# Layer 1 of a graph network: one column of source rows in seven selected by TensorE from node rows in SBUF in place of a gather

## The chip, the cores and the metric

The kernel runs on one core of a Trainium2 chip. Times are device microseconds of one execution; the median of ten executions before the change is 16345.49 us (16343.41 to 16347.37).

## The reference, cut to what matters

12500 nodes with 32 features, 400000 edges (src, dst), the edges sorted by dst. Three attention layers run over the edges, then a layer norm, then an edge network with a maximum over each node's edges, and a second layer norm. One attention layer is

```python
h = (x @ W.T).reshape(n, heads, ch)
a_s = (h * att_s[None]).sum(-1)
a_d = (h * att_d[None]).sum(-1)
logits = jax.nn.leaky_relu(a_s[src] + a_d[dst], neg_slope)
m = jax.ops.segment_max(logits, dst, num_segments=n)
ex = jnp.exp(logits - m[dst])
denom = jax.ops.segment_sum(ex, dst, num_segments=n)
alpha = ex / (denom[dst] + 1e-16)
out = jax.ops.segment_sum(alpha[:, :, None] * h[src], dst, num_segments=n)
```

with 2 heads of 16 channels in layers 1 and 2 and one head of 32 in layer 3. Layers 1 and 2 are followed by an elu and a clip at 3. What this case is about is `h[src]` and `a_s[src]`: for every edge, the row of its source node.

## The kernel before

The edges lie in dst order over 128 partitions, 3125 to a partition. Column t of a tile is edge t of every partition. The nodes are numbered p * 98 + c: 98 to a partition.

In front of the layers the kernel computes the rows of layer 1 for all nodes into `tb` (L354 to L364; 32 features, two logits, and the places of the node's last and first edge, 36 floats in all), writes them to `table1` in DRAM (L390), and finds each node's first and last edge with gathers of `found` in groups of up to 28 columns (L367 to L374). `empties` (L557) writes the rows of nodes without edges; it reads the biases.

`attention(li, idx)` goes through the edges in 54 chunks: 50 of 60 columns and the last of 48, 32, 29 and 16. For each chunk it

- gathers the source rows, one indirect DMA on POOL's queue for each column (L666 to L668, issued by the helper at L68), 128 rows a time, into a tile `g` from a pool of 4 buffers; in layer 1 from `table1`
- copies the places out of `g` (L683, L684), forms the logits (L695 to L698) and running maxima (L704) along the edges of a partition
- forms weights on ACT into `small_p` (L715), multiplies the rows by them (L723), and runs a segmented sum with scans over `gf` (L734)
- writes the sums (L736 to L739), divides by the denominator kept in `den`, adds the bias (`divided`, L494 to L501), and in layers 1 and 2 applies the elu and multiplies by the next layer's weights in blocks of 16 columns (`finish`, L510 to L534: L523 and L525 on DVE, L528 and L529 on PE, L531 and L532 on DVE), and writes the rows of the next layer's table (L744, L748)

What the scans hand from chunk to chunk stays in SBUF (`old`). After the last chunk of a layer the partitions' ends are merged (L751 to L784); layers 1 and 2 also issue 49 scatters of x each on POOL there (`move`, L624). `edge_network` (L805) has the same chunks, with gathers into `xs` at L834.

PSUM has eight tiles of 512 floats a partition. Before the change layer 1 uses `fixed` (biases in columns 0 to 127, `node_p` in 256 to 353 during the setup), `small_p` (weights in columns 0 to 119, `den` from 128), two for `rx`, one each for `pe` and `pa`, two for `ph`.

The instructions of an engine run in the order that the program was laid out in before it ran. This order isn't that of the source: independent instructions are put between dependent ones. Waits come from the tiles that instructions write and read.

Of the kernel before, what the change touches and what calls it, by code (L numbers as in the profile page):

```python
# [11 lines left out]
I32 = mybir.dt.int32  # L12
# [11 lines left out]
@with_exitstack  # L24
def gnn_resnorm_kernel(ctx: ExitStack, tc: tile.TileContext, a: dict, out: bass.AP):


# [36 lines left out]
    def bcast(ap, shape):  # L64
        return ap.to_broadcast(shape)
# [9 lines left out]
    def node_rows(table):  # L75
        return table[0:NN, :].rearrange("(p c) w -> p c w", c=NC)
# [4 lines left out]
    def empty_rows(table):  # L81
        return table[E:E + NN, :].rearrange("(p c) w -> p c w", c=NC)

    groups = [(c0, min(28, NC - c0)) for c0 in range(0, NC, 28)]

# [17 lines left out]
    gstack = ctx.enter_context(ExitStack())  # L103
    gpool = gstack.enter_context(tc.tile_pool(name="g", bufs=4, side="right"))
    early = ctx.enter_context(ExitStack())
    dpool = early.enter_context(tc.tile_pool(name="dst", bufs=1, side="right"))
    dst_i = dpool.tile([P, TE], I32, name="dst_i")
    nc.sync.dma_start(out=dst_i, in_=by_partition(a["dst"]))
    x0 = runs.tile([P, NC, D], F32, name="x0")
    nc.vector.memset(x0[96:P, REST:, :], 0.0)  # L110
    for p0, p1 in PIECES:
# [19 lines left out]
                   allow_small_or_imprecise_dtypes=True)  # L131
    fixed = ctx.enter_context(tc.tile_pool(name="fixed", bufs=1, space=PSUM)).tile([P, 512], F32, name="fixed")
    own = const.tile([P, 1], F32, name="own")
    nc.gpsimd.iota(own, pattern=[[1, 1]], base=E + NN, channel_multiplier=1,
                   allow_small_or_imprecise_dtypes=True)
    zeros = const.tile([P, 1250], F32, name="zeros")
    nc.vector.memset(zeros, 0.0)
# [57 lines left out]


    table1 = dram.tile([NN, D + 4], F32, name="table1")
    table_d = dram.tile([NN, 2], F32, name="table_d")
# [9 lines left out]
    def clear(table, part=0, parts=1):  # L208
        flat = edge_rows(table).rearrange("p t w -> p (t w)")
        k = TE * table.shape[1] // parts  # L210
        z = next(z for z in range(1250, 0, -1) if k % z == 0)
        tc.keep_in_program_order(
            nc.sync.dma_start(out=flat[:, part * k:part * k + k].rearrange("p (k z) -> p k z", z=z),
                              in_=bcast(zeros[:, None, :z], [P, k // z, z])))
# [82 lines left out]
    runs2 = ctx.enter_context(tc.tile_pool(name="runs2", bufs=1))  # L297
    cont = runs2.tile([P, TE + 1], F32, name="cont")
    src_last = runs2.tile([P, TE], I32, name="src_last")
    src_first = runs2.tile([P, TE], I32, name="src_first")  # L300
# [13 lines left out]
    with tc.tile_pool(name="seg", bufs=1) as sp, tc.tile_pool(name="rowsp", bufs=2) as rp, \  # L314
# [51 lines left out]

        for c0, n in groups:  # L367
            rows = rp.tile([P, 28, SB], I32, name="found")
            for c in range(n):
                gather(rows[:, c, :], dst_d, find_i[:, c0 + c:c0 + c + 1])  # L370
            less = rp.tile([P, 28, SB], BF16, name="less")[:, :n, :]
            nc.vector.tensor_tensor(less, rows[:, :n, :], bcast(node_p[:, c0:c0 + n, None], [P, n, SB]), op=ALU.is_lt)
            nc.vector.tensor_reduce(r[:, c0:c0 + n], less, axis=AX.X, op=ALU.add)
            nc.vector.tensor_add(first[:, c0:c0 + n], first[:, c0:c0 + n], r[:, c0:c0 + n])  # L374
# [9 lines left out]
        for col, place, index in ((D + 3, first, first_i), (D + 2, last, last_i)):  # L384
# [4 lines left out]
            nc.vector.tensor_copy(index, place)  # L389
        nc.sync.dma_start(out=node_rows(table1), in_=tb)  # L390

        nc.vector.memset(cont[:, 0:1], 0.0)
# [109 lines left out]

    def finish(li, pool, psum, den, v, n, hb=1):

        y = pool.tile([P, D * T], F32, name="y")[:, :D * n].rearrange("p (f t) -> p f t", t=n)
        divided(li, y, den, v, n)
# [10 lines left out]
        for b in range(0, n, TB):  # L517
# [7 lines left out]
            nc.vector.transpose(blocks(yt), yb.rearrange("p f t -> p t f"))  # L525
            ph = psum.tile([P, TB * D], F32, name="ph", bufs=hb)[:, :w]
            pa = psum.tile([P, TB * D], F32, name="pa")[:, :w]
            nc.tensor.matmul(ph, lhsT=w_bd, rhs=yt, start=True, stop=True)  # L528
            nc.tensor.matmul(pa, lhsT=a_bd, rhs=yt, start=True, stop=True)  # L529
            at = pool.tile([P, TB, D], F32, name="at")[:, :nt, :]  # L530
            nc.vector.transpose(tb[:, b:b + nt, :D], blocks(ph))  # L531
# [18 lines left out]
    def finish3(pool, psum, den, v, x, n):  # L550

        y = psum.tile([P, D * 64], F32, name="y3")[:, :D * n].rearrange("p (f t) -> p f t", t=n)
        divided(3, y, den, v, n)
        nc.vector.tensor_add(x, x, y.rearrange("p f t -> p t f"))
        layernorm(pool, den[:, 2 * T:], x, n)

    def empties():  # L557

        for table, r0 in (*((t, E + NN) for t in tables.values()), (gives[2], E), (gives[3], E)):
            w = (ROWS - r0) // P * table.shape[1]  # L560
            nc.sync.dma_start(out=table[r0:, :].rearrange("(p c) w -> p (c w)", p=P), in_=zeros[:, :w])
        with tc.tile_pool(name="empty", bufs=2) as ep, tc.tile_pool(name="emptyps", bufs=1, space=PSUM) as eps:
            for li in (1, 2):
# [15 lines left out]
    def turned(ap, rev):  # L579
        return ap[:, ::-1] if rev else ap  # L580
# [48 lines left out]
    def attention(li, idx):  # L629
# [9 lines left out]

        with tc.tile_pool(name=f"s{li}", bufs=2) as sp, tc.tile_pool(name=f"f{li}", bufs=2) as fp:  # L640
            if li > 1:
# [17 lines left out]
            with tc.tile_pool(name=f"ps{li}", bufs=1, space=PSUM) as psp, \  # L659
                    tc.tile_pool(name=f"fps{li}", bufs=1, space=PSUM) as fps:  # L660

                small_p = psp.tile([P, 512], F32, name="small_p")
                den = small_p[:, 128:]
                old = None
                for c, (t0, n) in enumerate(todo):
                    g = gpool.tile([P, T * (D + 4)], F32, name="g")[:, :n * w].rearrange("p (t w) -> p t w", w=w)  # L666
                    for t in range(n):
                        gather(g[:, t, :], table, idx[:, t0 + t:t0 + t + 1])  # L668
                    (ad, xr) = loaded
# [42 lines left out]
                    nc.vector.tensor_sub(lg, lg, mx[:, :, cur])  # L712
                    rx = psp.tile([P, heads, 512], F32, name="rx", bufs=3 - heads)
                    wt = small_p[:, :heads * n].rearrange("p (h t) -> p h t", t=n)
# [3 lines left out]
                    v = gf[:, :gw * (n + 1)].rearrange("p (f t) -> p f t", t=n + 1)  # L718
                    for h in range(heads):
                        nc.scalar.activation(  # L720
                            rx[:, h, :FS * (n + 1)].rearrange("p (k t) -> p k t", t=n + 1),
                            bcast(rr[:, h:h + 1, :], [P, FS, n + 1]), AF.Exp)
                        nc.vector.tensor_mul(v[:, h * wd:h * wd + ch, cur].rearrange("p f t -> p t f"),  # L723
                                             g[:, :, h * ch:(h + 1) * ch], bcast(wt[:, h, :, None], [P, n, ch]))
                        nc.scalar.copy(v[:, h * wd + ch, cur], wt[:, h, :])  # L725
                    if c == 0:
                        nc.vector.memset(v[:, :, carry:carry + 1], 0.0)
                    else:
                        nc.vector.tensor_copy(v[:, :, carry:carry + 1], old[0])
                    for h in range(heads):  # L730
                        for f in range(0, wd, FS):
                            k = min(FS, wd - f) * (n + 1)
                            o = (h * wd + f) * (n + 1)
                            nc.vector.tensor_tensor_scan(turned(gf[:, o:o + k], rev), turned(rx[:, h, :k], rev),  # L734
                                                         turned(gf[:, o:o + k], rev), 0.0, op0=ALU.mult, op1=ALU.add)
                    rows = sp.tile([P, T, gw + heads], F32, name="rows")[:, :n, :]  # L736
                    nc.scalar.copy(rows[:, :, :gw], v[:, :, cur].rearrange("p f t -> p t f"))  # L737
# [4 lines left out]
                    if li < 3:  # L742
                        tb, ta = finish(li, fp, fps, den, v[:, :, cur], n, hb=2)
                        nc.sync.dma_start(out=edge_rows(gives[li + 1])[:, t0:t0 + n, :], in_=ta)  # L744
                    else:
                        finish3(fp, fps, den, v[:, :, cur], xr, n)
                        tb = xr
# [57 lines left out]
    def edge_network(tag, in_order):  # L805


        with tc.tile_pool(name=f"in{tag}", bufs=2) as ip, tc.tile_pool(name=f"gx{tag}", bufs=4) as gp, \
                tc.tile_pool(name=f"v{tag}", bufs=2) as vp, tc.tile_pool(name=f"t{tag}", bufs=2) as tp, \
                tc.tile_pool(name=f"pf{tag}", bufs=1, space=PSUM) as pfp, \  # L810
                tc.tile_pool(name=f"ph{tag}", bufs=1, space=PSUM) as php:
            small_p = pfp.tile([P, 512], F32, name="small_p")
            todo = list(chunks(True))
# [17 lines left out]
            for c, (t0, n) in enumerate(todo):  # L831
                xs = gp.tile([P, T, D], F32, name="xs")
                for t in range(n):
                    gather(xs[:, t, :], tables[4], src_last[:, t0 + t:t0 + t + 1])  # L834
                xd, ea = loaded
# [57 lines left out]
                old = (xft[:, :, 0], first_v)  # L893
                z = vp.tile([P, T, D], F32, name="z", bufs=1)[:, :n, :]
                for f in range(0, D, FS):
# [62 lines left out]
```

## Time and profile before

| | us |
|---|---|
| median of 10 runs | 16345.49 |
| the profiled execution | 16347.18 |
| its span, first to last instruction | 16344.7 |
| gathers of layer 1 | 302.8 to 4234.2 |
| first and last landing of a chunk in layer 1 (L683) | 406.7, 4235.8 |
| first gather of layer 2 | 4300.2 |

By stage, from the window view: microseconds of the stretch, and busy microseconds of each engine.

| stretch | length | PE | DVE | ACT | POOL | granted clock |
|---|---|---|---|---|---|---|
| layer 1, 300 to 4235 | 3935 | 594.1 | 1474.2 | 808.6 | 2954.2 | 0.56 |
| layer 2, 4300 to 8205 | 3905 | 581.9 | 1412.9 | 789.4 | 2952.1 | 0.57 |
| layer 3, 8270 to 12180 | 3910 | 0.0 | 1387.4 | 503.2 | 2951.0 | 0.50 |
| edge network, 12222 to 16200 | 3978 | 1531.2 | 2394.0 | 734.4 | 2948.8 | 0.68 |
| one pitch of layer 1, 1969.2 to 2044.1 | 74.9 | 12.2 | 28.1 | 15.6 | 56.6 | 0.57 |

POOL's busy time is the issue of gathers and leaves out some 0.3 us between two of them. PE, DVE and ACT are the matrix, vector and scalar engines; PEld is PE's weight load, SP the queue of plain DMAs. The granted clock is that of PE, as a share of full speed. In a timeline line the columns are start, duration, engine, line of the kernel, operation, output and inputs, and in brackets the idle time before it and what ended it.

### The profile page before, as it was taken

How to read it: one execution, taken by the hardware profiler on the slowest of the kernel's cores; microseconds unless marked ns; L12 is line 12 of the kernel's file. 1: busy time of each engine (PE TensorE's matmuls, PEld its weight loads, DVE VectorE, ACT ScalarE, POOL GpSimd, SP SyncE). 2: the span in 40 equal slices, each digit the busy share in tenths (PEclk: the TensorE clock that was granted, in tenths of full speed). 3: DMA queues.
4: the chain of work that ended last, by engine and by line, in shares of the span. 5: the costliest groups of instructions: out<-in, count | busy, mean ns of one | idle time of the engine just before them, and what ended most of it. 6: DMA issues, size and time to landing. Idle time of an engine off the chain costs nothing.

```text
span 16344.7 us, 42394 instructions
## 1 busy us (share of the span) xinstructions
PE 2762.3 (17%) x5140; PEld 1118.3 (7%) x5140; DVE 6834.1 (42%) x9700; ACT 2898.9 (18%) x3835; POOL 12192.9 (75%) x12921
## 2 busy tenths in 40 slices
PE   0111111111111111111100000000003433334342
PEld 0000000000000000000000000000001111111110
DVE  2434333333334333333333333333335666665654
ACT  0212222121212122221211111111111111111111
POOL 6777777777777777777777777777767777777775
PEclk5555555555555555555555555555556666666676
DMA  4222222211111111111112222222222222222221
GB/s 60 76 55 73 55 58 71 55 48 43 43 41 47 41 47 41 44 44 41 47 49 56 51 58 51 56 53 56 53 57 59 66 66 64 67 65 64 69 63 42
DMA packets 580809, 897.64 MB, mean 55 GB/s; under 512 B 286270, under 2 KB 490237, under 8 KB 567069
## 3 DMA queue, kind: packets, MB, share of 16 engines
q1 hardware_dynamic: 167116, 665.01, 11.3%
q0 software_dynamic: 413088, 226.62, 9.6%
q10 hardware_dynamic: 304, 3.20, 0.1%
q14 instruction: 259, 2.12, 0.0%
q8 instruction: 42, 0.69, 0.0%
HBM read 390.67 MB, written 503.27 MB: 55 GB/s over the span
## 4 chain that ended last, share of the span: by engine, by line
POOL 71%; issue 23%; DMA 3%; DVE 1%; PE 0%; ACT 0%; POOLq 0%; DVEq 0%; ACTq 0%
POOL g L68 52%; POOL xs L68 17%; DMA g<-table,src_i 1%; DMA g<-table,src_first 1%; DMA g<-table,src_last 1%; DMA xs<-table,src_last 1%; POOL give L72 1%; POOL so L68 1%; POOL x_e L72 1%; PE ph L877 0%; DMA s<-sums,at_i 0%; PE pv L883 0%; DVE vf L887 0%; DVE z L803 0%; ACT xd L889 0%
## 5 line engine op out<-in xcount | busy, mean ns | idle before, releaser
L68 POOL DMA_INDIRECT g<-table,src_i x3125 | 2951.8, 945 | 979.9 <-issue 938.8
L68 POOL DMA_INDIRECT g<-table,src_last x3125 | 2950.7, 944 | 952.4 <-issue 937.5
L68 POOL DMA_INDIRECT xs<-table,src_last x3125 | 2948.6, 944 | 955.0 <-issue 936.2
L68 POOL DMA_INDIRECT g<-table,src_first x3125 | 2950.0, 944 | 952.4 <-issue 937.5
L697 DVE TENSOR_TENSOR lg<-g,af 128x60 f32<-128x60 f32 (+4 forms) x270 | 59.4, 250 | 4410.7 <-DMA g<-table,src_first 2327.0
L528 PE MATMUL ph<-yt,w_bd 128*128 128x512 f32 (+2 forms) x840 | 665.1, 887 | 3418.1 <-DVE yt L525 3412.1
L529 PE MATMUL pa<-yt,a_bd 128*128 128x512 f32 (+2 forms) x840 | 640.1, 857 | 3320.8 <-DVE at L532 3320.6
L877 PE MATMUL ph<-xt,wb_bd 128*128 128x512 f32 (+2 forms) x832 | 467.1, 646 | 2415.7 <-DVE xt L870 2415.7
L683 DVE CAST src_last<-g 128x60 int32<-128x60 f32 (+4 forms) x54 | 11.9, 221 | 2057.1 <-DMA g<-table,src_i 2057.1
L738 ACT COPY rows<-mx 128x120 f32<-128x120 f32 (+3 forms) x162 | 49.9, 308 | 4422.1 <-DVE mx L704 4368.9
L737 ACT COPY rows<-gf 128x2040 f32<-128x2040 f32 (+3 forms) x162 | 628.4, 3879 | 648.7 <-DVE gf L734 648.7
L734 DVE TENSOR_TENSOR_SCAN gf<-rx,gf 128x488 f32<-128x488 f32 (+4 forms) x918 | 732.2, 858 | 1.4 <-ACT gf L725 0.9
L591 PE MATMUL pt<-ident,tops 128*34 128x128 f32 (+1 forms) x3 | 1.0, 322 | 3948.5 <-DVE xr L548 3946.8
L723 DVE TENSOR_TENSOR gf<-g,small_p 128x960 f32<-128x960 f32 (+5 forms) x270 | 597.9, 2214 | 63.3 <-ACT small_p L715 63.2
L523 DVE SCALAR_TENSOR_TENSOR yb<-y,pe 128x512 f32<-128x512 f32 (+2 forms) x420 | 269.0, 640 | 605.2 <-ACT pe L521 586.7
L533 ACT COPY tb<-at 128x32 f32<-128x32 f32 (+4 forms) x420 | 92.3, 220 | 2314.0 <-DVE at L532 2314.0
L528 PEld LDWEIGHTS ph<-yt,w_bd 128*128 128x128 f32 x840 | 219.7, 289 | 3814.0 <-DVE yt L525 3344.1
L879 ACT ACTIVATE ht<-ph,b_c 128x512 f32<-128x512 f32 (+2 forms) x416 | 275.0, 661 | 1144.2 <-PE ph L877 1140.3
L529 PEld LDWEIGHTS pa<-yt,a_bd 128*128 128x128 f32 x840 | 220.8, 279 | 3689.0 <-DVE at L532 3516.0
L877 PE MATMUL ph<-et,wb_bd 128*128 128x512 f32 (+2 forms) x832 | 451.4, 627 | 0.0
L877 PE MATMUL ph<-xst,wb_bd 128*128 128x512 f32 (+2 forms) x832 | 430.8, 601 | 32.4 <-DVE xst L872 32.4
L883 PE MATMUL pv<-ht,w_bd 128*128 128x512 f32 (+2 forms) x832 | 415.1, 592 | 5.0 <-ACT ht L879 0.8
(295 smaller groups left out, 8583.5 us busy)
## 6 DMA issues: line engine op xcount, KB each, us to landing
sums<-rows SPq DMA_DIRECT2D x100, 1080.0 KB
table<-tb SPq DMA_DIRECT2D x50, 1020.0 KB
sums<-rows SPq DMA_DIRECT2D x50, 1020.0 KB
g<-table,src_i POOLq DMA_INDIRECT x3125
x_e<-zeros SPq DMA_DIRECT2D x10, 5000.0 KB
g<-table,src_last POOLq DMA_INDIRECT x3125
g<-table,src_first POOLq DMA_INDIRECT x3125
xs<-table,src_last POOLq DMA_INDIRECT x3125
```

The lines of the kernel that those rows point to most:

```text
L68: return nc.gpsimd.indirect_dma_start(out=dst, out_offset=None, in_=table, in_offset=bass.IndirectOffsetOnAxis(ap=idx, axis=0))
L72: return nc.gpsimd.indirect_dma_start(out=table, in_=src, in_offset=None, out_offset=bass.IndirectOffsetOnAxis(ap=idx, axis=0))
L523: nc.vector.scalar_tensor_tensor(yb, y[:, :, b:b + nt], 3.0, pe, op0=ALU.min, op1=ALU.add)
L528: nc.tensor.matmul(ph, lhsT=w_bd, rhs=yt, start=True, stop=True)
L529: nc.tensor.matmul(pa, lhsT=a_bd, rhs=yt, start=True, stop=True)
L533: nc.scalar.copy(tb[:, b:b + nt, D:], at[:, :, :heads])
L723: nc.vector.tensor_mul(v[:, h * wd:h * wd + ch, cur].rearrange("p f t -> p t f"), g[:, :, h * ch:(h + 1) * ch], bcast(wt[:, h, :, None], [ ...
L734: nc.vector.tensor_tensor_scan(turned(gf[:, o:o + k], rev), turned(rx[:, h, :k], rev), turned(gf[:, o:o + k], rev), 0.0, op0=ALU.mult, op1 ...
L737: nc.scalar.copy(rows[:, :, :gw], v[:, :, cur].rearrange("p f t -> p t f"))
L877: nc.tensor.matmul(ph, lhsT=wb_bd[:, s, h, :], rhs=x, start=(s == 1), stop=(s == 0))
L879: nc.scalar.activation(ht, ph, AF.Relu, bias=b1_c[:, h:h + 1])
L883: nc.tensor.matmul(pv, lhsT=w2_bd[:, h, :], rhs=hts[h], start=(h == 0), stop=(h == 1))
```

## The change

In layer 1, columns 6, 13, 20 and so on are not gathered (446 of 3125). Their rows are selected from the node rows, which stay in SBUF as `parts`: each float32 split into three bf16 terms, for 7 groups k of 14 nodes a partition, in the order (feature, node in group). For a selected column t, with source node = partition q, group k, place b within the group:

- two matmuls put q and 128 k of all 128 edges of the column, broadcast, into `places_p`, added up
- one compare of `places_p` with `kid` gives `oh`, for each k a 128 x 128 matrix of zeros and ones
- 7 x 3 matmuls of `oh` with `parts` add up in `acc`: for each edge the 14 rows of the group (504 floats)
- a product with the one-hot `bm` of b, and a sum over the 14, give the row, written into `g`

`places_p`, `small_p` and `den` are now columns of the tile `fixed`; `acc` has two buffers, `ph` one. The other layers and the edge network have the new code with nothing selected. To make room, `g` has 3 buffers, `xs` 3, `x0` lies in a pool of its own that ends with the gathers' pool, `y`, `at` and `rows` have one buffer, `zeros` is half as long, the product rows `z` go into `xs`, `rx` is one tile a head, and `found` is gathered in groups of 14.

```diff
+    KT, KN = 7, 14
+    EVERY = {1: 7, 2: 0, 3: 0, 4: 0}
...
-    gpool = gstack.enter_context(tc.tile_pool(name="g", bufs=4, side="right"))
+    xpool = gstack.enter_context(tc.tile_pool(name="x", bufs=1, side="right"))
+    gpool = gstack.enter_context(tc.tile_pool(name="g", bufs=3, side="right"))
...
+    small_p, places_p = fixed[:, 128:384], fixed[:, 384:]
...
+    kid = const.tile([P, KT], F32, name="kid")
+    nc.gpsimd.iota(kid, pattern=[[P, KT]], base=0, channel_multiplier=1, allow_small_or_imprecise_dtypes=True)
...
-    zeros = const.tile([P, 1250], F32, name="zeros")
+    zeros = const.tile([P, 625], F32, name="zeros")
...
+    def split(pool, k, rows, w):
+        rows = rows.rearrange("p b w -> p w b")
+        hi, mid, lo = (parts[:, i, k, :KN * w].rearrange("p (w b) -> p w b", b=KN) for i in range(3))
+        r = pool.tile([P, D + 4, KN], F32, name="rest")[:, :w, :]
+        nc.scalar.copy(hi, rows)
+        nc.vector.tensor_sub(r, rows, hi)
+        nc.scalar.copy(mid, r)
+        nc.vector.tensor_sub(r, r, mid)
+        nc.scalar.copy(lo, r)
+
+    class Fetch:
+        def __init__(self, stack, name, every, w):
...
+            m = TE // every
+            self.at = pool.tile([P, 2, m], BF16, name="fat", bufs=1)
+            self.b = pool.tile([P, m], F32, name="fb", bufs=1)
+            with tc.tile_pool(name=f"{name}t", bufs=1) as fp:
+                node, q, r, k = (fp.tile([P, m], F32, name=x) for x in ("fn", "fq", "fr", "fk"))
+                q_i = fp.tile([P, m], I32, name="fi")
+                nc.vector.tensor_copy(node, src_i[:, :m * every].rearrange("p (i c) -> p i c", c=every)[:, :, every - 1])
+                divide(q, r, node, NC, q_i, k)
+                nc.vector.tensor_copy(self.at[:, 0, :], q)
+                divide(k, self.b, r, KN, q_i, q)
+                nc.vector.tensor_scalar(self.at[:, 1, :], k, float(P), None, op0=ALU.mult)
...
+        def fetch(self, psum, g, t, to, bufs=2):
+            if t not in self:
+                return
+            pool, w, i = self.pool, self.w, t // self.every
+            for j in range(2):
+                nc.tensor.matmul(places_p, lhsT=bcast(self.at[:, j, i:i + 1], [P, P]), rhs=ident_b,
+                                 start=(j == 0), stop=(j == 1))
+            oh = pool.tile([P, KT, P], BF16, name="oh")
+            nc.vector.tensor_tensor(oh, bcast(places_p[:, None, :], [P, KT, P]), bcast(kid[:, :, None], [P, KT, P]),
+                                    op=ALU.is_equal)
+            bm = pool.tile([P, KN], F32, name="bm")
+            nc.vector.tensor_scalar(bm, count[:, :KN], self.b[:, i:i + 1], None, op0=ALU.is_equal)
+            acc = psum.tile([P, 512], F32, name="acc", bufs=bufs)[:, :KN * w]
+            for k in range(KT):
+                for part in range(3):
+                    nc.tensor.matmul(acc, lhsT=oh[:, k, :], rhs=parts[:, part, k, :KN * w],
+                                     start=(k == part == 0), stop=(k == KT - 1 and part == 2))
+            mine = pool.tile([P, D + 4, KN], F32, name="mine")[:, :w, :]
+            nc.vector.tensor_mul(mine, acc.rearrange("p (w b) -> p w b", b=KN), bcast(bm[:, None, :], [P, w, KN]))
+            nc.vector.tensor_reduce(g[:, to, :w], mine, axis=AX.X, op=ALU.add)
...
         nc.sync.dma_start(out=node_rows(table1), in_=tb)
+        for k in range(KT):
+            split(tp, k, tb[:, k * KN:(k + 1) * KN, :], D + 4)
...
-    def finish(li, pool, psum, den, v, n, hb=1):
-        y = pool.tile([P, D * T], F32, name="y")[:, :D * n].rearrange("p (f t) -> p f t", t=n)
+    def finish(li, pool, psum, den, v, n):
+        y = pool.tile([P, D * T], F32, name="y", bufs=1)[:, :D * n].rearrange("p (f t) -> p f t", t=n)
...
-            ph = psum.tile([P, TB * D], F32, name="ph", bufs=hb)[:, :w]
+            ph = psum.tile([P, TB * D], F32, name="ph")[:, :w]
...
-                small_p = psp.tile([P, 512], F32, name="small_p")
                 den = small_p[:, 128:]
...
                     for t in range(n):
-                        gather(g[:, t, :], table, idx[:, t0 + t:t0 + t + 1])
+                        if t0 + t not in fetch:
+                            gather(g[:, t, :], table, idx[:, t0 + t:t0 + t + 1])
+                    for t in range(n):
+                        fetch.fetch(psp, g, t0 + t, t)
...
-                    rx = psp.tile([P, heads, 512], F32, name="rx", bufs=3 - heads)
...
                     for h in range(heads):
+                        rx = psp.tile([P, 512], F32, name="rx", bufs=heads)
...
-                    rows = sp.tile([P, T, gw + heads], F32, name="rows")[:, :n, :]
+                    rows = sp.tile([P, T, gw + heads], F32, name="rows", bufs=1)[:, :n, :]
...
-                z = vp.tile([P, T, D], F32, name="z", bufs=1)[:, :n, :]
+                z = xs[:, :n, :]
```

## The prediction

> **What bounds the kernel now.** I read the page's busy line and the chain that ended last first, then the costliest group of instructions.
>
> ```profile
> PE 2762.3 (17%) x5140; PEld 1118.3 (7%) x5140; DVE 6834.1 (42%) x9700; ACT 2898.9 (18%) x3835; POOL 12192.9 (75%) x12921
> ...
> POOL 71%; issue 23%; DMA 3%; DVE 1%; PE 0%; ACT 0%; POOLq 0%; DVEq 0%; ACTq 0%
> ...
> L68 POOL DMA_INDIRECT g<-table,src_i x3125 | 2951.8, 945 | 979.9 <-issue 938.8
> ```
>
> The end is set by one queue. In layer 1 each gather takes 945 ns on POOL and 300 ns pass before the next ("issue" idle, 938.8 us over 3125): 1.248 us each. The chain in order of time shows the same as a pitch between the landings that end two chunks of 60:
>
> ```profile
> 2044.09 2.32 DMA g<-table,src_i
> ...
> 2119.06 2.34 DMA g<-table,src_i
> ```
>
> 74.9 us = 60 x 1.248. Next the timeline of one chunk of layer 1, to see how much of that pitch the other engines use:
>
> ```profile
> 2055.41 0.21 DVE L683 CAST src_last<-g 128x60 int32<-128x60 f32 x1 [38.18 <-DMA g<-table,src_i]
> ...
> 2071.13 4.69 DVE L734 TENSOR_TENSOR_SCAN gf<-rx,gf 128x488 f32<-128x488 f32 x6
> ...
> 2079.43 2.15 DVE L501 TENSOR_TENSOR y<-y,fixed 128x1920 f32<-128x1920 f32 x1
> 2081.62 1.90 ACT L510 ACTIVATE e<-y,minus 128x1920 f32<-128x1920 f32 x1 [1.71 <-DVE y L501]
> ...
> 2087.89 0.69 DVE L523 SCALAR_TENSOR_TENSOR yb<-y,pe 128x512 f32<-128x512 f32 x1 [6.30 <-ACT pe L521]
> ```
>
> DVE stood idle 38.18 us for the gathers. In a full pitch DVE is busy 28.1 us and PE 12.2 us. So there is room beside POOL; the question is whether the new work can stand there.
>
> **Removed.** Every seventh column, 3125 // 7 = 446 gathers x 1.248 = 557 us of POOL. A full chunk holds 8.57 selected columns on average, so POOL needs 51.43 x 1.248 = 64.2 us a chunk. Were POOL still the bound, the profiled execution (span 16344.7, time 16347.18) would come to about 15,790.
>
> **Added per selected column.** PE: two 128-column bf16 matmuls (places_p), then 21 of 504 columns into acc. DVE: oh (896 elements), bm (14), mine (504), the reduce (504). Rates of PE:
>
> ```profile
> L335 PE MATMUL p_all<-under,is_hi x25: 241/286/287, 40.5 to 42.5; 128*128 128x99 bf16 x25
> ```
> ```profile
> 45.70 0.42 PE L357 MATMUL pt<-ident,x 128*128 128x128 f32 x1
> ...
> 46.91 0.27 PE L357 MATMUL pt<-ident,x 128*128 128x128 f32 x1
> ```
> ```profile
> 14479.26 1.91 PE L877 MATMUL ph<-et,wb_bd 128*128 128x512 f32 x2
> ...
> 14488.29 1.02 PE L877 MATMUL ph<-xst,wb_bd 128*128 128x512 f32 x2
> ...
> 14489.15 1.02 PE L877 MATMUL ph<-xt,wb_bd 128*128 128x512 f32 x2
> ```
> ```profile
> 2064.00:2067.00 3.00, 1.39 (x5) 0.68 (x4) 2.74 (x9) 1.52 (x5) 2.26 (x3) 1.00 0.12 15
> ```
>
> The 25 bf16 matmuls run 24 steps in 2.0 us, 84 ns for 99 columns, 0.84 ns a column. That is before the clock rose: equal transposes take 0.42 us at 45.7 and 0.27 at 46.9. An f32 pair of 512 columns is paced 1.71 us before the rise (14479.26 to 14480.97) and 0.86 after it (14488.29 to 14489.15), half. So a 504-column bf16 matmul is 0.42 us slow and 0.212 fast; a burst of 21 is 8.9 or 4.45 us. In that last burst the rise came about 4.5 us after its first matmul. The window row has clock 1.00 although PE stood still 1.6 us in it, so I take the fast pace for all but the first 4.5 us of a chunk's selection (2.2 us lost).
>
> One sentence of the page "TensorE: Matmul & The Clock Gate" (Back-to-back issue gap) speaks otherwise: a sustained stream at 512 columns would go at about 131 ns a matmul. An estimate by that figure: a burst of 2.75 us, a step 14.6 us shorter than the one I come to below, and a time about 16,015, faster than now. The f32 pair above, four times 0.215, does not show that pace.
>
> DVE rows:
>
> ```profile
> L327 DVE TENSOR_TENSOR is_hi<-count,hi 128x3200 bf16<-128x3200 f32 x1 | 3.5, 3487 | 0.0
> ```
> ```profile
> L802 DVE TENSOR_TENSOR vf<-vf,xp 128x480 f32<-128x480 f32 x108 | 70.6, 653 | 37.3 <-ACT xp L897 37.3
> ...
> L540 DVE TENSOR_REDUCE small_p<-z 128x60 f32<-128x1920 f32 x27 | 58.3, 2161 | 0.9
> ```
>
> At 1.09 ns an element oh is 1.0 to 1.05 us; mine 0.68; the reduce at 1.12 ns about 0.6; bm 0.1 in start-to-start terms. Together 2.4 us, 20 us a chunk: DVE 28 + 20 = 48, PE 12 + 8.57 x 4.75 = 53, both under 64.2. By busy time alone the change would be free.
>
> **Where it stands.** By order it isn't. places_p is a slice of fixed, and so now is small_p (weights, den); layer 1's bias, read by L501, lies there too. The trace shows what a shared tile of that size does:
>
> ```profile
> 169.32 1.98 DVE L372 TENSOR_TENSOR less<-found,fixed 128x1750 bf16<-128x1750 int32 x1 [9.93 <-DMA found<-dst_d,find_i]
> ...
> 171.33 0.27 ACT L451 COPY fixed<-b_all 128x128 f32<-128x128 f32 x1 [114.48 <-DVE less L372]
> ```
>
> ACT writes columns 0 to 127, DVE reads 256 to 353, and ACT waits 114.48 us for that read. So places_p of chunk c+1 must wait for L501 of chunk c, the last reader of fixed; and chunk c+1 can't begin (L683 reads all of g) before its last selected column is reduced. The page "PSUM — Partial Sum Buffer" (PSUM bank collisions raise a hardware error) has it as a rule: guard by bank and not by address. Were the ordering by address only, the selection could run beside the previous chunk, and the time would be the 15,790 above; the row agrees with the page.
>
> So a step is A + F. **A**, from L683 to the end of L501: 26.2 us in the timeline, of which 9.2 are transposes and their PE waits of the previous chunk's finish, put between; 17.0, and 17.5 with a little more for ACT. **F**, the selection of 8.57 columns. PE takes the places of the next column behind the burst of this one; then mine must wait for acc (0.27 for drain and semaphore; a 512-column record is 1.02 long at a pace of 0.86), mine 0.6, oh 1.05, 0.05 to PE: 2.0 us without a burst; 2.6 if the reduce goes before oh as well. I take 2.2, nearer to the first because independent DVE work is often put between two dependent instructions in the timeline. 6.65 us a column, 57.0 a chunk. To it: 2.2 for the slow clock; the finish of chunk c, whose tail now runs in F: its PE work is 6.4 us at the fast pace, half outside the gaps, 3.2; its 11 us of DVE in front of mine or oh now and then, 3. F = 65.4, step 82.9 us against 74.9. POOL, at 64.2, runs ahead until the three g buffers are full.
>
> Landing of the first chunk to that of the last: 49 x 82.9 = 4062; the four short chunks: A 52.8, 18 columns x 6.65 = 120, the rest 17.5 = 190. 4252 against 3829 now (406.7 to 4235.8). Chunk 0 starts later: its selection waits for the last bias read of empties, whose DVE work now lies in two parts, 25 us up to 333 and 24 us behind L683; together from 308 to 358, then Fetch's setup (some 22 DVE instructions of 446 elements, 11 us) and F, to 434 in place of 406.7, +27. The 37 scatters (46 us on POOL) behind the last gather now run while POOL is ahead: the way from last gather to layer 2's first, 66 us, falls to the 48 of layer 3, which has none: -18. Sum 423 + 27 - 18 = +432: 16,779 for that execution, and 1.7 less for the median, rounded: **16,780**.
>
> **At nothing.** split's 35 instructions on ACT and DVE lie in the 126.7 us that DVE waits for the places gather (else 25 us once). Found in groups of 14 ends with the same 14 as now. Clears in rows of half the length go through SP's queue; DMA is 18% busy in a pitch (else 20 us). One ph, y, at and rows buffer, g and xs pools of 3, z in xs: in layers 2 and 3 DVE works 1413 and 1387 of some 3905 us, and a z is written 35 us after its landing while its buffer is next gathered into after 150; without that cover some 5 us at each layer's end.
>
> **Bounds.** Low: gap 1.5 (oh before mine), the finish wholly in the gaps: F = 8.57 x 5.95 + 2.2 = 53.2, step 70.7, loop 3629, first landing +15: 16,140. High: A 20, gap 2.9, finish PE wholly outside and half its DVE: F 77, step 97, loop 4978, first landing +39: 17,520.
>
> **Rivals.** (1) Faster: the selection hides. It decides once A + F is under 74.9, that is with a gap below 1.27 us a column at my other terms, and wholly if selection runs beside A; POOL at 64.2 is the floor, 15,790. For it: 38 us of idle DVE and the busy sums; against it the row at 171.33. 0.13 for the floor. (2) The clock falls between bursts: burst 8.9, 11.1 a column, F 105, step 122.6, loop 6281, first landing +67: 18,850. For it: 0.56 mean clock in layer 1; against it the 1.00 across a gap of 1.6 us; mine are longer. 0.07.
>
> **Chances.** The serial loop at the fast clock has 0.80, of which 0.09 lies under the time now. No change within 0.2% (33 us, about what a measurement of this kernel can tell) gets 0.03: faster 0.22, same 0.03, slower 0.75. The range is the serial loop's own, 16,100 to 17,500; outside lie rival 1 below and rival 2 above.
>
> **What would show it.** Landings of L683 in layer 1 83 us apart; DVE's wait there no longer on a gather but on PE's acc; POOL idle before gathers for the release of g; bursts of about 4.5 us with gaps near 2 in PE; first places matmul of a chunk right after L501. The forecast is wrong if bursts run during A, if POOL never waits, or if bursts are nearer 9 us.

## The result and the profile after

The changed kernel takes 16929.0 us (median of 8 runs, 16928.5 to 16930.19); the kernel before took 16345.18 beside it. The ratio is 1.0357, interval 1.0348 to 1.0366: slower by 584 us, where 16,780 was forecast, 435 slower. The profiled execution has a span of 16926.7.

The page after: the busy line, the chain by engine, and three of the costliest groups.

```profile
PE 4784.8 (28%) x15398; PEld 2026.7 (12%) x15398; DVE 7951.7 (47%) x11529; ACT 2912.1 (17%) x3856; POOL 11775.5 (70%) x12476
...
POOL 53%; issue 18%; PE 13%; DVE 11%; DMA 3%; ACT 1%; DVEq 0%; POOLq 0%; ACTq 0%
...
L71 POOL DMA_INDIRECT g<-table,src_i x2679 | 2530.4, 945 | 1920.4 <-DVE gf L817 1083.0
L262 PE MATMUL acc<-parts,oh 128*128 128x504 bf16 x9366 | 2181.4, 391 | 631.4 <-DVE oh L255 631.4
...
L265 DVE TENSOR_TENSOR mine<-acc,bm 128x504 f32<-128x504 f32 x446 | 303.9, 681 | 1571.3 <-PE acc L262 1570.6
```

446 gathers are gone and POOL's busy time fell by 417 us, yet the chain has passed from POOL (71% to 53%) to PE and DVE (1% to 24%). POOL now stands idle 1083.0 us for DVE's L817, the reader that gives a g buffer back: the gathers run ahead and are held up. DVE waits 1570.6 us for the selection's accumulators, PE 631.4 for DVE's one-hot rows. The two engines wait for each other in turn, the mark of a serial loop.

One step of layer 1, DVE in the timeline (start, duration, line, operation, what ended the idle time):

```profile
2027.18 0.20 DVE L773 CAST src_last<-g 128x60 int32<-128x60 f32 x1
...
2042.28 2.15 DVE L585 TENSOR_TENSOR y<-y,fixed 128x1920 f32<-128x1920 f32 x1
...
2062.91 1.05 DVE L255 TENSOR_TENSOR oh<-fixed,kid 128x896 bf16<-128x896 f32 x1
...
2115.02 0.20 DVE L773 CAST src_last<-g 128x60 int32<-128x60 f32 x1
```

PE in the same step:

```profile
2044.50 0.39 PE L252 MATMUL fixed<-ident_b,fat 128*128 128x128 bf16 x2 [18.80 <-DVE y L585]
2046.08 7.12 PE L262 MATMUL acc<-parts,oh 128*128 128x504 bf16 x21 [1.19 <-DVE oh L255]
...
2064.02 4.64 PE L262 MATMUL acc<-parts,oh 128*128 128x504 bf16 x21
...
2070.43 4.64 PE L262 MATMUL acc<-parts,oh 128*128 128x504 bf16 x21 [1.66 <-DVE oh L255]
...
2108.90 4.64 PE L262 MATMUL acc<-parts,oh 128*128 128x504 bf16 x21 [1.66 <-DVE oh L255]
```

PE stands idle 18.80 us through the chunk's own work and starts the next places when the bias add L585 ends. Nine bursts follow. From the second on they are 6.41 us apart; between the first and the second lie 17.94, because the first runs at the slow clock and because DVE does the finish of the chunk before (L607 to L616) ahead of the second one-hot. Then the next landing: 87.84 us for nine columns, and at the mean of 8.57 columns 87.84 - 0.43 x 6.41 = 85.1; the mean of the 49 steps between full chunks is 84.9. Before, it was 74.9.

### The profile page after: what moved, and what is told of

Read it like the earlier page. It is cut to its first block, busy times and chain, and to the rows that moved or that the text cites. A ratio compares the mean times of both kernels' runs of the same rounds, so it can differ in the third digit from the quotient of the medians.

```text
span 16926.7 us, 65312 instructions
## 1 busy us (share of the span) xinstructions
PE 4784.8 (28%) x15398; PEld 2026.7 (12%) x15398; DVE 7951.7 (47%) x11529; ACT 2912.1 (17%) x3856; POOL 11775.5 (70%) x12476
## 4 chain that ended last, share of the span: by engine, by line
POOL 53%; issue 18%; PE 13%; DVE 11%; DMA 3%; ACT 1%; DVEq 0%; POOLq 0%; ACTq 0%
POOL g L71 35%; POOL xs L71 16%; PE acc L262 12%; DVE oh L255 2%; DVE mine L265 1%; DVE gf L823 1%; DVE gf L817 1%; PE ph L612 1%; DVE yt L609 1%; DMA g<-table,src_first 1%; DMA g<-table,src_last 1%; DVE y L581 1%; DMA xs<-table,src_last 1%; DVE y L585 1%; POOL so L71 1%
## 5 line engine op out<-in xcount | busy, mean ns | idle before, releaser
L71 POOL DMA_INDIRECT g<-table,src_i x2679 | 2530.4, 945 | 1920.4 <-DVE gf L817 1083.0
L262 PE MATMUL acc<-parts,oh 128*128 128x504 bf16 x9366 | 2181.4, 391 | 631.4 <-DVE oh L255 631.4
L262 PEld LDWEIGHTS <-oh 128*128 128x128 bf16 x9366 | 908.6, 101 | 1789.9 <-DVE oh L255 732.7
L612 PE MATMUL ph<-yt,w_bd 128*128 128x512 f32 (+2 forms) x840 | 547.8, 741 | 1813.5 <-DVE yt L609 1740.9
L265 DVE TENSOR_TENSOR mine<-acc,bm 128x504 f32<-128x504 f32 x446 | 303.9, 681 | 1571.3 <-PE acc L262 1570.6
L613 PE MATMUL pa<-yt,a_bd 128*128 128x512 f32 (+2 forms) x840 | 525.3, 714 | 1754.4 <-DVE at L616 1754.1
L817 DVE TENSOR_TENSOR gf<-g,fixed 128x960 f32<-128x960 f32 (+5 forms) x270 | 601.6, 2228 | 67.4 <-ACT fixed L804 65.3
L607 DVE SCALAR_TENSOR_TENSOR yb<-y,pe 128x512 f32<-128x512 f32 (+2 forms) x420 | 268.3, 639 | 559.2 <-ACT pe L605 548.5
L255 DVE TENSOR_TENSOR oh<-fixed,kid 128x896 bf16<-128x896 f32 x446 | 481.2, 1079 | 25.9 <-PE fixed L252 25.9
L973 PEld LDWEIGHTS ph<-xt,wb_bd 128*128 128x128 f32 x832 | 172.0, 215 | 2624.0 <-DVE xt L966 2420.4
```

The source lines that it names most:

```text
L71: return nc.gpsimd.indirect_dma_start(out=dst, out_offset=None, in_=table, in_offset=bass.IndirectOffsetOnAxis(ap=idx, axis=0))
L255: nc.vector.tensor_tensor(oh, bcast(places_p[:, None, :], [P, KT, P]), bcast(kid[:, :, None], [P, KT, P]), op=ALU.is_equal)
L262: nc.tensor.matmul(acc, lhsT=oh[:, k, :], rhs=parts[:, part, k, :KN * w], start=(k == part == 0), stop=(k == KT - 1 and part == 2))
L265: nc.vector.tensor_mul(mine, acc.rearrange("p (w b) -> p w b", b=KN), bcast(bm[:, None, :], [P, w, KN]))
L607: nc.vector.scalar_tensor_tensor(yb, y[:, :, b:b + nt], 3.0, pe, op0=ALU.min, op1=ALU.add)
L973: nc.tensor.matmul(ph, lhsT=wb_bd[:, s, h, :], rhs=x, start=(s == 1), stop=(s == 0))
```

## The experiments

In the tables of this part "loop" is from the first to the last landing of src_last in layer 1, in the profiled execution:

| kernel | columns selected in a full chunk | first landing | loop | time | ratio, interval |
|---|---|---|---|---|---|
| before | 0 | 406.7 | 3829.1 | 16345.2 | 1 |
| after | 8.57 | 499.1 | 4362.1 | 16929.0 | 1.0357, 1.0348 to 1.0366 |
| none | 0 | 430.0 | 3831.1 | 16365.7 | 1.0006, 0.9995 to 1.0018 |
| every14 | 4.29 | 481.6 | 3513.1 | 16092.1 | 0.9835, 0.9807 to 0.9864 |
| two_parts | 8.57 | 496.7 | 3815.9 | 16401.5 | 1.0010, 0.9999 to 1.0020 |
| own_bank | 8.57 | 511.6 | 3811.5 | 16393.3 | 1.0023, 1.0012 to 1.0034 |
| acc_places | 8.57 | 503.3 | 3314.2 | 15896.1 | 0.9715, 0.9687 to 0.9744 |
| acc_empty2 | 8.57 | 502.0 | 3314.7 | 15909.6 | 0.9709, 0.9693 to 0.9725 |
| empty2 | 8.57 | 506.0 | 4362.3 | 16947.5 | 1.0343, 1.0322 to 1.0363 |
| acc6_again | 10 | 516.2 | 3673.7 | 16265.0 | 0.9945, 0.9928 to 0.9961 |

Each ratio is against runs of the kernel before taken beside it; their median was 16345.2 (after), 16356.4 (none, every14, own_bank, acc_places), 16385.4 (two_parts, empty2, acc_empty2) and 16355.6 (acc6_again).

**The other edits alone.** Nothing is selected; the smaller buffers, shared tiles, split and the groups of 14 stay.

```diff
-    EVERY = {1: 7, 2: 0, 3: 0, 4: 0}
+    EVERY = {1: 0, 2: 0, 3: 0, 4: 0}
```

> All other edits of the change, with no column selected (the node rows are still split). My theory, a serial loop of chunk work (17.25 us) and selection (6.41 us a column and 12.9 us a chunk): without columns nothing is serial, POOL bounds layer 1 again with 74.9 us a chunk, and the time is that of before, 16345, within 20 us; the slow single-buffered empties are hidden since POOL gathers ahead into three buffers. The rival, that the smaller pools and the shared PSUM tile cost: a good part of the +584 us stays, 16450 or more.

16365.7, ratio 1.0006. Where nothing is selected, the edits that were costed at nothing cost nothing that can be measured: the loss comes with the selection. What the smaller buffers cost beside a selection this run can't show.

**Half as many columns.**

```diff
-    EVERY = {1: 7, 2: 0, 3: 0, 4: 0}
+    EVERY = {1: 14, 2: 0, 3: 0, 4: 0}
```

> One column in fourteen, 223. Serial loop: selection 4.29 x 6.41 + 12.9 = 40.4, with 17.25 of chunk work 57.7 us, below POOL's 55.7 x 1.248 = 69.5 us. So POOL bounds, the step falls from 74.9 to 69.5, and the time is 16345 - 278 = 16067, up to 16100 with the later start. The rival, a cost in proportion to the selected columns (a slower gather or contention for each): half the loss, about 16640.

16092.1, faster than the kernel before and within the 16067 to 16100 expected. Three landings of DVE in its timeline:

```profile
2033.98 0.21 DVE L773 CAST src_last<-g 128x60 int32<-128x60 f32 x1 [14.34 <-DMA g<-table,src_i]
...
2102.67 0.21 DVE L773 CAST src_last<-g 128x60 int32<-128x60 f32 x1 [6.91 <-DMA g<-table,src_i]
...
2172.62 0.21 DVE L773 CAST src_last<-g 128x60 int32<-128x60 f32 x1 [13.78 <-DMA g<-table,src_i]
```

DVE waits for gathers again, and the mean of these two steps, 69.3, is POOL's 55.71 x 1.248 = 69.5. The serial loop is still there, but at 17.25 + 12.9 + 4.29 x 6.41 = 57.6 us (the terms are taken apart below) it is now shorter than the gathers, which set the pace. The layer's first four steps show it alone: POOL is still ahead there, no landing waits for a gather, and they take 55.3 to 61.7 us.

**The places out of the shared tile.** In own_bank they get a PSUM tile of their own, for which the accumulator has to give up its second buffer. In acc_places they are written into the first 128 columns of the column's own accumulator, which has two buffers; the matmuls that follow overwrite them.

```diff
 own_bank
+            places_p = psum.tile([P, P], F32, name="places_p")
             for j in range(2):
                 nc.tensor.matmul(places_p, ...
...
-            acc = psum.tile([P, 512], F32, name="acc", bufs=bufs)[:, :KN * w]
+            acc = psum.tile([P, 512], F32, name="acc", bufs=1)[:, :KN * w]
```
```diff
 acc_places
+            acc = psum.tile([P, 512], F32, name="acc", bufs=bufs)
+            places_p, acc = acc[:, :P], acc[:, :KN * w]
             for j in range(2):
                 nc.tensor.matmul(places_p, ...
...
-            acc = psum.tile([P, 512], F32, name="acc", bufs=bufs)[:, :KN * w]
```

> Places in a PSUM tile of their own with one buffer, and acc with one buffer. Only the wait for the last reader of fixed is gone; places still wait for oh of the column before, so the gap stays at 1.96 us or grows. If the shared tile alone makes the loop serial: first places matmul of a chunk ahead of the bias add, step between 67.9 (selection alone) and 85.1, time 16090 to 16900. If the order of priorities keeps selection behind the chunk work: 16929 or slower.

> The two places matmuls write into the column's own acc tile (two buffers) and no longer into fixed. Theory: their order behind the last reader of fixed and behind oh of the column before is gone. The places of the next column can go ahead of this column's burst, the gap between bursts of 1.96 us shrinks to some 0.3 us, 4.75 us a column: step 17.25 + 8.57 x 4.75 + 12.9 = 70.9, time 16929 - 49 x 14.2 = 16230; with selection beside the chunk work as well down to POOL's 64.2 a step, 15905. The rival, that the order comes from the program's order of priorities and not from the shared tile: 16929 within 30 us.

16393.3 and 15896.1. The timeline of own_bank, one step of eight columns:

```profile
2004.14 0.20 DVE L774 CAST src_last<-g 128x60 int32<-128x60 f32 x1
2008.04 0.28 PE L253 MATMUL places_p<-ident_b,fat 128*128 128x128 bf16 x2
2017.75 6.95 PE L263 MATMUL acc<-parts,oh 128*128 128x504 bf16 x21 [9.44 <-DVE oh L256]
2021.05 2.14 DVE L586 TENSOR_TENSOR y<-y,fixed 128x1920 f32<-128x1920 f32 x1
...
2026.47 4.64 PE L263 MATMUL acc<-parts,oh 128*128 128x504 bf16 x21 [1.66 <-DVE oh L256]
...
2074.87 0.21 DVE L774 CAST src_last<-g 128x60 int32<-128x60 f32 x1
```

The places (2008.04) and the first burst of the next chunk (2017.75) now start before the bias add (2021.05), which they didn't in the shared tile. With a single accumulator only this one column goes ahead. The step is 70.73 where eight columns of the changed kernel take 87.84 - 6.41 = 81.43; over 49 steps the mean is 74.4 against 84.9, 10.5 less. In acc_places:

```profile
1989.40 0.21 DVE L774 CAST src_last<-g 128x60 int32<-128x60 f32 x1
...
2002.65 11.07 PE L263 MATMUL acc<-parts,oh 128*128 128x504 bf16 x42 [7.80 <-DVE oh L257]
...
2034.14 9.10 PE L263 MATMUL acc<-parts,oh 128*128 128x504 bf16 x42 [0.73 <-DVE oh L257]
2045.02 9.10 PE L263 MATMUL acc<-parts,oh 128*128 128x504 bf16 x42 [0.73 <-DVE oh L257]
...
2057.33 0.43 DVE L774 CAST src_last<-g 128x60 int32<-128x60 f32 x1
```

Two columns go as one run of 42 matmuls, 10.88 us a pair instead of 12.82, and one pair runs in the chunk's own work. POOL's waits there:

```profile
POOL g L71 <- DVE gf L818: 46.1, 2, 24.1
```

It waits for a buffer 46.1 us in all (two waits, both behind 3660 us, at the layer's end) instead of 1083.0. The removed gathers come out: 460 us under the kernel before beside it. This doesn't make POOL the only bound again. The mean step is 64.8 us, POOL's gathers take 64.2, and from 1000 to 3500 us no landing waits for a gather; DVE's longest wait in layer 1 is for the selection's accumulators:

```profile
DVE mine L266 <- PE acc L263: 786.8, 308, 3.0
```

So the places wait behind the last reader of *any* column of the shared tile: they stand in its columns 384 to 511, and L585 reads columns 0 to 127. The Trainium skill, page "PSUM — Partial Sum Buffer" (PSUM bank collisions raise a hardware error), has the rule to guard PSUM by bank and not by address; the order seen here agrees with it. What the shared tile alone cost is what own_bank gave back, 536 us. The other 497 of the 1033 that acc_places gave back come on top, with two buffers for the places, through which two columns go as one run.

**A third less matmul.** The low part of each number is left out.

```diff
-                for part in range(3):
+                for part in range(2):
...
-                                     start=(k == part == 0), stop=(k == KT - 1 and part == 2))
+                                     start=(k == part == 0), stop=(k == KT - 1 and part == 1))
```

> The changed kernel with the low bf16 part left out of the selection: 14 selecting matmuls a column instead of 21; the result is short of the third part of each number. Theory (the bursts stand on the path one for one, since a chunk's selections can't start before the bias add of the chunk before): a burst 14 x 0.212 = 2.97 us, a column 4.93 instead of 6.41 (the gap of 1.96 stays), so a step is shorter by 8.57 x 1.48 = 12.7 us, 49 steps: 16929 - 622 = 16,307. Rival (the step is set by VectorE's order or by gaps, and TensorE's bursts lie beside it): 16,800 or more, with the column pitch at 6 us or over.

16401.5. The first, third and fourth burst of a chunk in its PE timeline:

```profile
2151.68 5.41 PE L262 MATMUL acc<-parts,oh 128*128 128x504 bf16 x14 [1.19 <-DVE oh L255]
...
2174.32 3.15 PE L262 MATMUL acc<-parts,oh 128*128 128x504 bf16 x14 [2.19 <-DVE oh L255]
2179.24 3.15 PE L262 MATMUL acc<-parts,oh 128*128 128x504 bf16 x14 [1.66 <-DVE oh L255]
```

The pitch is 4.92 against 6.41, as the theory has it. The time fell by 546 against empty2, which equals the changed kernel within about 0.1% and ran beside it; 622 was expected. Of the 76 missing, some 60 lie, by the step shown, in the first two columns of the 49 steps: 22.64 us from the first burst to the third, 24.35 in the changed kernel, so 1.7 less and not 3.0. What stands there is DVE's finish, and a shorter burst doesn't shorten it.

**The start.** The changed kernel has one buffer for the work on empty rows where there were two.

```diff
-        with tc.tile_pool(name="empty", bufs=1) as ep, ...
+        with tc.tile_pool(name="empty", bufs=2) as ep, ...
```

> The changed kernel with the pool for empty rows at two buffers again, as before the change. Theory (the single buffer makes each empty chunk wait for the writes of the one before it: the first landing of layer 1 is late by 92 us against 27 forecast): first landing at 435 to 440 instead of 499, the rest alike, 16,865 to 16,875. Rival (the start is set by something else of the change, the split and packing): first landing stays at 490 or later and the time at 16,920 to 16,935.

> The places in the column's own accumulator tile (two buffers), and the pool for empty rows at two buffers: both costs of the change mended at once. Theory: 15,896 - 60 = 15,835, faster than the kernel before by 500 us; the step stays at POOL's 64 us. Rival (the late start only lets gathers queue that then run ahead, so that it is caught up within layer 1): 15,890 to 15,900.

A miss, both times: the first landing stays (506.0 and 502.0), and so does the time. DVE's timeline of empty2 names the reason:

```profile
407.28 1.09 DVE L654 TENSOR_TENSOR z<-x,fixed 128x896 f32<-128x896 f32 x1 [64.79 <-DMA table<-z]
...
440.57 0.59 DVE L237 CAST fn<-src_i 128x446 f32<-128x446 int32 x1 [2.54 <-DMA table<-z]
```

and that of the kernel before:

```profile
406.71 0.21 DVE L683 CAST src_last<-g 128x60 int32<-128x60 f32 x1 [73.08 <-DMA g<-table,src_i]
...
435.78 0.18 DVE L545 TENSOR_SCALAR sm<-sm 128x14 f32<-128x14 f32 x1
481.29 0.21 DVE L683 CAST src_last<-g 128x60 int32<-128x60 f32 x1 [45.33 <-DMA g<-table,src_i]
```

With either number of buffers the empty rows wait for their writes until some 400 us (with one buffer, in the changed kernel, ACT waits 33.43 us for them until 399.92). Before, the 29 us that remain then (406.95 to 435.96) lay behind the first landing, in DVE's wait for the second chunk. Now the first landing comes after the selection, and the selection after its setup (L237), which comes behind all of them and waits for their last write (2.54 us above).

**Controls and more columns.** acc1 is the changed kernel with one accumulator buffer (the second edit of own_bank alone). every6, acc6 and acc5 select every sixth or fifth column, without and with the places in the accumulator; mine has one buffer, so that they fit.

```diff
-    EVERY = {1: 7, 2: 0, 3: 0, 4: 0}
+    EVERY = {1: 6, 2: 0, 3: 0, 4: 0}
...
-            mine = pool.tile([P, D + 4, KN], F32, name="mine")[:, :w, :]
+            mine = pool.tile([P, D + 4, KN], F32, name="mine", bufs=1)[:, :w, :]
```

> The changed kernel with one accumulator buffer for the selection in place of two; the places stay in the shared tile. A control for own_bank, which also had one. Theory (the next column's one-hot rows already come after the product of this column in VectorE's order, so the second buffer is never used ahead): no change, 16,910 to 16,950, column pitch 6.41. Rival (the second buffer carries work, so own_bank's gain is the shared tile's less something): 17,000 or more.

> The changed kernel with every sixth column selected instead of every seventh (520 in place of 446, ten a full chunk); the product tile mine has one buffer so that it fits. Theory (each selected column stands on the path with its whole pitch of 6.41 us, and the other 30.2 us of a step do not grow with their number): a step of 94.3, 74 x 6.41 = 474 more, 17,403, although POOL issues 74 gathers fewer. Rival (the 12.9 us of the selection beside the columns grow with them too): 17,500 or more. Rival (POOL's gathers still count): below 17,340.

> acc_places with every sixth column selected; one buffer for mine. Theory (POOL is the bound there again, 1.248 us a gather): 74 gathers fewer, 92 us, 15,805. Rival (TensorE and VectorE, ten columns with 4.75 us of TensorE each beside 12 us of other work, are the bound by now): 15,890 or more.

> acc_places with every fifth column selected (625, twelve a chunk); one buffer for mine. Theory: TensorE's 12 x 4.75 + 12.2 = 69.2 us a chunk are over POOL's 48 x 1.248 = 59.9, the bound passes to TensorE and the step grows from 64.4 to about 69: 15,896 + 49 x 4.8 = 16,130. Rival (POOL still the bound): 15,896 - 223 = 15,673.

Beside these four the kernel before itself took 18567.9, over 13% more than everywhere else, and the four took 22500.7, 22854.5, 22168.4 and 22632.8. The chain of acc1 shows where part of the time went:

```profile
POOL 29%; issue 18%; DVE 17%; PE 16%; another core or an unknown queue 16%; ACT 3%; DMA 0%; DVEq 0%; ACTq 0%; POOLq 0%; SPq 0%
```

16% of the span waits for something that the profile puts on another core or an unknown queue; the profiles of the other three have 15 to 20% of it, and no other profile here has any. What it was is not known. The times expected of acc1, every6 and acc5 stay open. One thing can be read in spite of it, the pitch of acc1's bursts where nothing intrudes:

```profile
2484.94 4.64 PE L262 MATMUL acc<-parts,oh 128*128 128x504 bf16 x21 [1.67 <-DVE oh L255]
...
2491.35 4.64 PE L262 MATMUL acc<-parts,oh 128*128 128x504 bf16 x21 [1.67 <-DVE oh L255]
```

6.41, as with two buffers. So the single buffer in own_bank didn't change its column; what moved there is the start.

> The kernel of acc6 once more, since in the call of acc6 the kernel before itself took 18,568. Theory (POOL is the bound): 15,896 - 74 x 1.248 = 15,805 where the kernel before takes 16,350. Rival (TensorE and VectorE bind at ten columns a chunk): 15,890 or more.

16265.0: the theory fell, by 460. Its landings:

```profile
2025.15 0.20 DVE L774 CAST src_last<-g 128x60 int32<-128x60 f32 x1
...
2096.85 0.20 DVE L774 CAST src_last<-g 128x60 int32<-128x60 f32 x1
...
2168.52 0.20 DVE L774 CAST src_last<-g 128x60 int32<-128x60 f32 x1
```

71.7 us a step, where POOL needs 50 x 1.248 = 62.4, and POOL waits for DVE's L818 again (532.0 us in all). Five pairs at 10.88 are 54.4, which leaves 17.3 for the chunk's work and the finish. If these 17.3 stay, 8.57 columns come to 46.6 + 17.3 = 63.9, beside POOL's 64.2 and the 64.8 measured: acc_places sits where the two bounds meet. Of the two shares tried with the places in the accumulator, one column in seven is the better. It is the fastest version that ran, 15896.1 us.

## Why the prediction was right, point by point

- **The reason.** The forecast said that places of a chunk wait for the bias add of the one before, since both lie in one PSUM tile. The first places matmul follows L585 in the trace (18.80 us idle before it), and in own_bank, with the places in a tile of their own, they start ahead of the bias add and 536 us come back. Shown.
- **The chunk's own work**, 17.5 us forecast: 17.25 from L773 to the end of L585 (2115.02 to 2132.27). Right.
- **The column**, 6.65 forecast: 6.41. The pace of 0.212 us a matmul holds: 42 in a run take 9.10 us and 21 take 4.64, so 21 more take 4.46. The 131 ns that the Trainium skill, page "TensorE: Matmul & The Clock Gate" (Back-to-back issue gap), has for a sustained stream at 512 columns were not seen at 504 columns. The gap is 1.96 against 2.2: the reduce goes behind the next one-hot, not before it.
- **The rest of the selection**, 2.2 + 3.2 + 3 = 8.4 us forecast: 85.1 - 17.25 - 8.57 x 6.41 = 12.9. The term is mis-sized by 4.5. The slow clock takes 2.5 (7.12 against 4.64; 2.2 forecast). The finish, with 6.2 forecast, takes 9.0: it was thought to fall partly into the gaps, and stands instead almost whole between the first burst and the second, where 17.94 - 6.41 = 11.5 us lie beyond the usual pitch, 2.5 of them the clock. The last 1.4 are the ends, from L585 to the first burst and from the last burst to the landing (1.65 + 6.12 - 6.41), which the forecast left out.
- **The step** came to 84.9 (85.1 by these terms) instead of 82.9 and the loop to 4362 instead of 4252: 99 of these 110 are the 49 steps, the rest the four short chunks, 201 instead of 190.
- **The first landing**, +27 forecast: +92.4. Of the three terms this one was furthest off for its size. "Together from 308 to 358" counted the busy time of the empty rows' layer norm and not their waits for writes. It runs to 431.5, and the wait for its last write to 433.7; the setup then takes 11.0, as forecast, and the selection 54.4. Nor is it the bias read in the shared tile that holds the selection there: in acc_places, which has no places in that tile, the first landing is as late (503.3), and the first places matmul waits for the setup's L239.
- **The end of the layer**, -18 forecast: the last landing to layer 2's first gather fell from 64.4 to 28.2, -36.2. The gather of `s` on POOL started 45.5 us after the last landing, among the scatters (4281.27), and now starts 8.8 after it (4870.04). Why that makes twice the forecast was not tried.
- The sum of the three is +533 + 92.4 - 36.2 = +589 against +432; the span grew by 582. The end's error covers 18 us of the other two.
- **At nothing**: none shows it for these edits without a selection, ratio 1.0006.
- **Rival 1**, the hidden selection at 15,790, fails in this kernel because the places wait for the bias add. Without that wait, and with two buffers for the places, acc_places comes within 106 us of it: 15896.1.
- **Rival 2**, the clock that falls between bursts. The windows of one step's selection and of the whole loop (length, then busy time and count of PE, PEld, DVE, ACT and POOL, granted clock, DMA share, GB/s):

```profile
2044.50:2112.00 67.50, 51.13 (x217) 22.24 (x218) 31.10 (x49) 9.46 (x15) 42.80 (x46) 0.95 0.16 40
499.00:4861.00 4362.00, 2579.37 (x10902) 1113.78 (x10902) 2509.49 (x4264) 809.32 (x1152) 2448.25 (x2594) 0.87 0.19 50
```

The clock is 0.95 in a selection, and only the first burst is slow: it falls in the chunk's work and not between bursts. The busy sums are as forecast too: 2509 / 51.3 steps is 48.9 us of DVE a step (48 forecast), and 50.3 of PE (53). No engine is full; the order makes the time.

## What to carry to other kernels

Before work is moved to an idle engine, look for the tile through which it is tied to the work it should run beside. In this kernel the users of a shared PSUM tile are ordered by the whole tile, and moving 128 columns of scratch into another tile that was there anyway, and had two buffers, turned 584 us of loss into 460 of gain. Where several queues are near balance, sum each one's serial order and not only its busy time, and try more than one share of the work to move: in the shared tile 4.29 columns a chunk left POOL the bound and 8.57 did not; out of it 8.57 stood where the two bounds meet, and 10 beyond. And at the start of a stage look at what an instruction waited for, not only at how long it worked: what had been covered by a wait may come to stand in front of it.

## What was not expected of the hardware

The granted clock stays up not only across gaps of 1.96 us, but through the 11 us between the first and the second burst, which hold only the finish's matmuls, with idle times of at most 1.82 us between them: it is 1.00 from 2053.2 to 2064.0, and the second burst takes 4.64 us like all later ones. After the 18.80 us of the chunk's own work it has fallen (0.50 from 2044.5 to 2051.0), and the first burst takes 7.12. In acc_places 7.80 us of idle are enough: the clock is 0.50 from 2002.6 to 2005.6, and the run of 42 takes 11.07 us instead of 9.10.
